# Routing a LoRA gate: one of two small products goes through DRAM, the other takes the whole array in float32r

## The chip, the cores and the metric

The kernel runs on one core of one Trainium2 chip. The core has a matrix engine (TensorE, PE in the profile, with its weight loads under PEld), VectorE (DVE), ScalarE (ACT), GpSimd (POOL) and SyncE (SP), which here does nothing but issue transfers in order. The metric is the time of one execution on the device, in microseconds (us).

## The reference, cut to what matters

For 128 slices x of 128 tokens by 1024 features the reference computes a graph attention step and then a LoRA mixture of experts, each added to its input:

```python
x = x + gnn(layernorm(x), adj, adj, W, a)
x = x + ffn(layernorm(x), router_w, lora_down, lora_up)
# gnn: Wh = h @ W per head (16 heads of 64); att = softmax over columns of
#      leaky_relu(Wh1 + Wh2), masked by adj == 0, times adj; elu(att @ Wh)
# ffn, E = 8 experts of rank R = 16, the 2 best of each slice by its first token:
gates = softmax(top2(y[:, 0, :] @ router_w.T))          # one pair per slice
down = einsum('blh,erh->bler', y, lora_down)
out  = y + einsum('bler,ehr,be->blh', down, lora_up, gates)   # y is the layernorm
```

Each slice uses two experts, and so 2 x 16 = 32 of the 128 LoRA rows. Which two, and with which weights, is known only at run time.

## The kernel before, in words

The slices are taken in 64 pairs (index `q`) and in 32 groups of 4 slices (index `g`, two pairs each). For each pair `project` (L390) computes the product with W in seven products of halves (Strassen's scheme with shared sums), each of 8 float32 matmuls of 128x128 by 260 columns, all on line L417, into two double banks of PSUM. The loop from L835 puts the work of the other stages into eight gaps before, between and after these seven products: every engine gets its instructions in exactly the order in which this loop calls the functions; no scheduler changes it. The gaps hold, for the pair before, the attention (`attend` L534 on TensorE, `update` L544 to L553 on VectorE and ScalarE), its statistics, and the transposing of its result: `turn` copies it into `halves` on ScalarE (L584) and SyncE issues a transposing transfer into `tt` (L586); `rejoin` (L590) copies `tt` into `y_t`.

The expert stage runs per group. In the first of a group's rounds `logits` (L614, L617) multiplies the group's four first tokens by the router, and `choose` finds the two best experts on VectorE. In its second round:

- `fetch` (gap 0, ahead of the first product) tells every LoRA row's partition its expert. The partition's number is 32 x slice + 16 x choice + rank, and the experts' numbers stand on four partitions, one per slice. `spread` (L649) puts them on the diagonal of a 4 x 8 array, and `to_rows` (L670) multiplies ones (4 x 128) by it, so that all eight numbers of the group reach all 128 partitions in `pb`. A mask `slot` (L672) and a sum (L674) pick a partition's own. From `pb` come eight columns of row numbers (L682) for the eight gathers of `down` and one (L685) for the gather of `up`, all on GpSimd (L688, L692).
- `weigh` (end of gap 0) turns the two logits into two gates per slice, on four partitions (L661 to L663), and spreads them in the same way.
- `gates` (gap 3, between the third and the fourth product) takes them to the 128 partitions by a second product on L670, with mask and sum.
- `ffn_down` (gap 4, L707) multiplies the gathered rows by `y_t`, and ScalarE reads the result out into `dn`, times the gate of each partition (L713). `ffn_up` (gaps 5 and 6, L723) multiplies `dn` by the gathered `up`; VectorE adds it to x (L727), and SyncE stores the slice (L730).

So both users of L670 stand in TensorE's stream between products of L417: the first between the seventh product of one pair and the first of the next, the second between the third and the fourth. Tiles of the tag `hp` (`hp`, `halves`, `nz`) share two buffers, and PSUM tiles of the tag `pm` (`pl`, `pb`, `ph`, `pd`, `pu`) four. On SyncE's queue a round begins with the loads of the next pair (L101 for `xt`, L96 for x), then come the two transposes of L586, and then the stores. The last group takes another way (`down_dense`, `gates_dense`, `up_dense`) that uses neither product of L670, so there are 31 of each.

Of the kernel before, what the change touches and what calls it, by code (L numbers as in the profile page):

```python
# [8 lines left out]
F32 = mybir.dt.float32  # L9
F32R = mybir.dt.float32r  # L10
# [4 lines left out]
ALU = mybir.AluOpType  # L15
AX = mybir.AxisListType
# [9 lines left out]
def adj_ffn_kernel(  # L26
# [15 lines left out]
    nc = tc.nc  # L42
    B, N, D = x.shape
    P = 128
# [6 lines left out]
    R = ER // E  # L51
    TOP = 2
    GR = TOP * R
    HALF = 512
# [3 lines left out]
    NG, _, G, _ = adj.shape  # L58
# [5 lines left out]
    const = ctx.enter_context(tc.tile_pool(name="const", bufs=1))  # L64
    work = ctx.enter_context(tc.tile_pool(name="work", bufs=2))
    small = ctx.enter_context(tc.tile_pool(name="small", bufs=3))
    ps_w = ctx.enter_context(tc.tile_pool(name="ps_w", bufs=2, space=bass.MemoryType.PSUM))
    ps_m = ctx.enter_context(tc.tile_pool(name="ps_m", bufs=4, space=bass.MemoryType.PSUM))
# [7 lines left out]
    GRP = {}  # L76


    dram = ctx.enter_context(tc.tile_pool(name="dram", bufs=1, space=bass.MemoryType.DRAM))
# [63 lines left out]
    mean_of, sum_of = (work.tile([P, P], F32, tag="dn", name=n) for n in ("mean_of", "sum_of"))  # L143
# [6 lines left out]
    ident = const.tile([P, P], F32, name="ident")  # L150
# [2 lines left out]
    nc.vector.memset(half_pow, -0.5)  # L153
    fold = small.tile([P, H], F32, tag="fold", name="fold", bufs=1)
    nc.vector.tensor_reduce(fold, ident.rearrange("p (t h) -> p h t", t=KH)[:, 0:H], AX.X, ALU.add)
    ones_g = const.tile([G, P], F32, name="ones_g")
    nc.vector.memset(ones_g, 1.0)

    order = const.tile([G, E], F32, name="order")
    for e in range(E):  # L160
# [121 lines left out]
    slot = down_row = up_row = None  # L282

    def experts(part):

        nonlocal slot, down_row, up_row
        pr = ps_m.tile([P, HALF], F32, tag="pm", name="pr")
        nc.tensor.matmul(pr[:, 0:E + ER], sum_of, part, start=True, stop=True)
        for t, lo, n in ((router_sb.rearrange("p k e -> p e k"), 0, E),
                         (down_sb.rearrange("p e r k -> p (e r) k"), E, ER)):  # L290
            nc.vector.tensor_tensor(t, t, pr[:, lo:lo + n, None].to_broadcast([P, n, KC]),
                                    ALU.subtract)
        nc.sync.dma_start(table.rearrange("(e p) c -> p e c", p=P),
                          down_sb.rearrange("p e r k -> p e (r k)"))

        slot = const.tile([P, 1, G * TOP], F32, name="slot")
        nc.vector.tensor_reduce(slot[:, 0], ident.rearrange("p (j r) -> p j r", r=R), AX.X,
                                ALU.add)
        rows = work.tile([P, P], I32, tag="hp", name="rows")
        nc.gpsimd.iota(rows, pattern=[[0, G * TOP], [1, R]], base=E * R, channel_multiplier=0)  # L300
        at_r = work.tile([P, P], F32, tag="hp", name="at_r")
        nc.vector.tensor_tensor(at_r, rows, ident, ALU.mult)
        up_row = const.tile([P, 1], F32, name="up_row")
        nc.vector.tensor_reduce(up_row, at_r, AX.X, ALU.add)
        row = small.tile([P, 1], I32, tag="row", name="row", bufs=1)
        nc.gpsimd.iota(row, pattern=[[0, 1]], base=E * P, channel_multiplier=1)
        down_row = const.tile([P, 1], F32, name="down_row")
        nc.vector.tensor_copy(down_row, row)
# [311 lines left out]
    def choose(g):  # L620

        st = GRP[g]
        both = small.tile([G, E + 1], F32, tag="lg", name="lg")
        nc.vector.tensor_copy(both, st["pl"][:G, 0:E + 1])
        lg, dev = both[:, 0:E], both[:, E:E + 1]
        top = small.tile([G, 8], F32, tag="top", name="top")
        nc.vector.max(out=top, in_=lg)

        val = small.tile([G, 2, TOP], F32, tag="val", name="val")
        first = small.tile([G, E], F32, tag="first", name="first")  # L630
        mark = small.tile([G, 2, E], F32, tag="mark", name="mark")
        for s in range(TOP):
            nc.vector.scalar_tensor_tensor(mark[:, s], lg, top[:, s:s + 1], order,
                                           op0=ALU.is_equal, op1=ALU.mult)
            if s:
                nc.vector.tensor_scalar(first, order, val[:, 0, 0:1], None, op0=ALU.is_equal)
                nc.vector.scalar_tensor_tensor(mark[:, s], first, float(-E), mark[:, s],
                                               op0=ALU.mult, op1=ALU.add)
            nc.vector.tensor_reduce(val[:, 0, s:s + 1], mark[:, s], AX.X, ALU.max)
        if g < NG - 1:  # L640
            st["experts"] = spread(val[:, 0], "experts")
        pr = small.tile([G, 2], F32, tag="pr", name="pr")
        nc.vector.tensor_sub(pr[:, 0:1], top[:, 1:2], top[:, 0:1])
        st.update(val=val, pr=pr, dev=dev)

    def spread(val, name):

        own = small.tile([G, G, TOP], F32, tag=name, name=name)
        nc.vector.tensor_tensor(own, ident[:G, :G, None].to_broadcast([G, G, TOP]),  # L649
                                val[:, None, :].to_broadcast([G, G, TOP]), ALU.mult)  # L650
        return own.rearrange("g t s -> g (t s)")

    def ratio(g):
        st = GRP[g]
# [2 lines left out]
    def weigh(g):  # L657

        st = GRP[g]
        gate, pr = st["val"][:, 1], st["pr"]  # L660
        nc.vector.tensor_scalar(gate[:, 0:1], pr[:, 1:2], 1.0, None, op0=ALU.add)  # L661
        nc.vector.reciprocal(gate[:, 0:1], gate[:, 0:1])
        nc.vector.tensor_mul(gate[:, 1:2], pr[:, 1:2], gate[:, 0:1])  # L663
        if g < NG - 1:
            st["gates"] = spread(gate, "gates")

    def to_rows(own, name):

        pb = ps_m.tile([P, HALF], F32, tag="pm", name="pb")
        nc.tensor.matmul(pb[:, 0:G * TOP], ones_g, own, start=True, stop=True)  # L670
        mine = small.tile([P, G * TOP], F32, tag="mine", name="mine")
        nc.vector.tensor_tensor(mine, pb[:, 0:G * TOP], slot[:, 0], ALU.mult)  # L672
        of_slot = small.tile([P, 1], F32, tag=name, name=name)
        nc.vector.tensor_reduce(of_slot, mine, AX.X, ALU.add)  # L674
        return pb, of_slot

    def fetch(g):

        st = GRP[g]
        pb, mine = to_rows(st["experts"], "of_slot")  # L680
        at_down = small.tile([P, G * TOP], U32, tag="at_down", name="at_down")
        nc.vector.tensor_scalar(at_down, pb[:, 0:G * TOP], float(-P), down_row, op0=ALU.mult,  # L682
                                op1=ALU.add)
        at_up = small.tile([P, 1], U32, tag="at_up", name="at_up")
        nc.vector.tensor_scalar(at_up, mine, float(-R), up_row, op0=ALU.mult, op1=ALU.add)  # L685
        st["down"] = work.tile([P, G * TOP * R, KC], F32, tag="down", name="down", bufs=1)
        for j in range(G * TOP):
            nc.gpsimd.indirect_dma_start(  # L688
                out=st["down"][:, j * R:(j + 1) * R].rearrange("p r k -> p (r k)"), out_offset=None, in_=table,
                in_offset=bass.IndirectOffsetOnAxis(ap=at_down[:, j:j + 1], axis=0))  # L690
        st["up"] = work.tile([P, D], F32, tag="up", name="up", bufs=1)
        nc.gpsimd.indirect_dma_start(  # L692
            out=st["up"], out_offset=None, in_=up_t,
            in_offset=bass.IndirectOffsetOnAxis(ap=at_up[:, 0:1], axis=0))

    def gates(g):

        st = GRP[g]
        st["gate"] = to_rows(st["gates"], "gate")[1]

    def ffn_down(g):

# [132 lines left out]
    for q in range(NQ + 2):  # L835
        gaps = [[] for _ in range(8)]
        if q == 0:
            prepare(gaps)
        g, part = divmod(q - 2, 2)
        ffn = 0 <= g < NG  # L840
        if ffn and not part:
            gaps[6] += [(logits, g), (choose, g)]
# [3 lines left out]
        if ffn and not part:  # L846
            gaps[6].append((ratio, g))
            if g == NG - 1:
                gaps[6] += [(down_dense, g, 3, 1), (weigh, g)]
# [27 lines left out]
        if ffn and part and g == NG - 1:  # L877
            gaps[0] += [(gates_dense, g), (up_dense, g)]
        elif ffn and part:
            gaps[0].insert(0, (fetch, g))  # L880
            gaps[0].append((weigh, g))
            gaps[3].insert(0, (gates, g))
            gaps[4].insert(0, (ffn_down, g))
            gaps[5].insert(0, (ffn_up, (g, 0)))
            gaps[6].append((ffn_up, (g, 1)))
# [14 lines left out]
        if q == 1:  # L900
            gaps[0].append((squares_of, 1))
            gaps[5].append(keep("tables", table_parts))
            gaps[7].append(keep("", experts, "tables"))
# [50 lines left out]
```

## Time and profile before

| | |
|---|---|
| time, median of 3 runs | 1949.1 us (1949.08 to 1950.11) |
| span of the profiled run | 1947.3 us |
| TensorE busy | 1931.7 us, 99% |
| VectorE busy | 1638.3 us, 84% |
| ScalarE busy | 1089.6 us, 56% |
| GpSimd busy | 832.7 us, 43% |
| TensorE's share of the chain that ended last | 95% |
| granted clock of TensorE | 0.996 of full |

A line of the profile's groups gives the source line, the engine, the operation, output and input, the array's rows and columns in use for a matmul, the moving operand's shape, then the count, the busy time in us, the mean ns of one, and the idle time of the engine just before them with what ended it. A line of the timeline gives the start in us, how long a run of equal instructions took, the instruction, how many of it were merged, and in brackets the idle time before it. Matmuls overlap in their pipeline: the time of one record is a latency, and the distance from one to the next is what it costs.

### The profile page before, as it was taken

To read this page: it belongs to the slowest core of one execution; us is meant where nothing else is said; L and a number is where in the kernel's file an instruction comes from. 1 tells how busy PE (TensorE), PEld (TensorE's weight loads), DVE (VectorE), ACT (ScalarE), POOL (GpSimd) and SP (SyncE) were. 2 spreads that over 40 slices of the span, in tenths; PEclk is the share of its full clock that TensorE was granted. 3 is DMA by queue.
4 is the path that set the end of the run, shared out by engine and by line. 5 is a ranking of instruction groups with operands and counts; after the bars stand their busy time and mean duration, and the time that the engine had idled before them with its cause. 6 is when DMAs were issued, how large, how long until landed. Compare 5 with 4: busy or idle time off the path is not lost.

```text
span 1947.3 us, 30291 instructions
## 1 busy us (share of the span) xinstructions
PE 1931.7 (99%) x11096; PEld 1574.6 (81%) x11096; DVE 1638.3 (84%) x3477; ACT 1089.6 (56%) x1060; POOL 832.7 (43%) x1135
## 2 busy tenths in 40 slices
PE   9999999999999999999999999999999999999997
PEld 6878888888888888888888888888888888888885
DVE  6888888888988888888888888888888888888886
ACT  3656556556555556555555565565555555555653
POOL 3345433355444355333454433553444553334540
PEclk9999999999999999999999999999999999999998
DMA  7455655665655656556557556556556565565452
GB/s 302 133 184 142 183 172 153 187 176 136 197 175 152 190 151 164 182 159 179 184 130 194 171 151 188 167 148 193 170 163 185 146 174 176 154 187 182 125 165 95
DMA packets 343955, 329.25 MB, mean 169 GB/s; under 512 B 274304, under 2 KB 276352, under 8 KB 343296
## 3 DMA queue, kind: packets, MB, share of 16 engines
q1 hardware_dynamic: 326080, 285.35, 50.1%
q0 software_dynamic: 17008, 40.91, 7.3%
q8 instruction: 88, 1.44, 0.3%
q10 hardware_dynamic: 720, 1.06, 0.1%
q14 instruction: 59, 0.48, 0.1%
HBM read 193.57 MB, written 67.63 MB: 134 GB/s over the span
## 4 chain that ended last, share of the span: by engine, by line
PE 95%; DVE 2%; ACT 1%; DMA 0%; issue 0%; POOL 0%; POOLq 0%; DVEq 0%; ACTq 0%
PE pw L417 80%; PE ph L534 6%; PE pu L723 3%; PE pd L707 3%; PE pb L670 1%; PE pl L614 1%; PE pu L784 1%; DMA tt<-halves 0%; DVE xn L553 0%; DVE hp L544 0%; DVE xn L552 0%; PE idle L149 0%; DVE stats L314 0%; ACT xn L606 0%; DVE parts L490 0%
## 5 line engine op out<-in xcount | busy, mean ns | idle before, releaser
L417 PE MATMUL pw<-w_sb,xt 128*128 128x260 f32 (+1 forms) x4080 | 944.4, 386 | 0.0
L417 PEld LDWEIGHTS pw<-w_sb,xt 128*128 128x128 f32 x4080 | 764.7, 190 | 144.7 <-issue 24.6
L417 PE MATMUL pw<-w_sb,s 128*128 128x260 f32 (+1 forms) x3072 | 711.1, 384 | 1.9 <-DVE u L425 1.9
L417 PEld LDWEIGHTS pw<-w_sb,s 128*128 128x128 f32 x3072 | 578.1, 190 | 115.7 <-issue 22.8
L318 POOL TENSOR_SCALAR rstd<-mv 128x2 f32<-128x2 f32 x126 | 27.4, 218 | 851.3 <-DVE mv L315 846.1
L590 ACT COPY y_t<-tt 128x2048 uint16<-128x2048 uint16 x126 | 313.1, 2505 | 67.3 <-DMA tt<-halves 67.1
L688 POOL DMA_INDIRECT down<-table,at_down x248 | 251.5, 1014 | 163.0 <-DVE e L508 89.4
L314 DVE BATCH_NORM_STATS2 stats<-xn 128x6 f32<-128x512 f32 x504 | 318.8, 674 | 0.1
L584 ACT COPY halves<-xn 128x2048 uint16<-128x2048 uint16 x126 | 239.3, 1899 | 141.0 <-DVE xn L553 141.0
L486 ACT ACTIVATE parts<-wh,rstd 128x512 fp32r<-128x512 f32 x192 | 134.1, 716 | 213.8 <-DVE wh L425 213.8
L551 ACT ACTIVATE ex<-hp 128x1024 f32<-128x1024 f32 x128 | 135.3, 1057 | 177.4 <-DVE hp L544 177.4
L727 DVE SCALAR_TENSOR_TENSOR xn<-pu,rstd,xn 128x512 f32<-128x512 f32 x248 | 169.0, 744 | 21.9 <-PE pu L723 21.9
L544 DVE TENSOR_TENSOR hp<-ph,att 128x512 f32<-128x512 f32 x256 | 161.3, 671 | 10.3 <-PE ph L534 10.0
L553 DVE SCALAR_TENSOR_TENSOR xn<-ex,xn 128x1024 f32<-128x1024 f32 x128 | 156.8, 1225 | 14.2 <-DVE xn L552 0.9
L534 PE MATMUL ph<-parts,adj_f 128*128 128x512 f32 x512 | 164.5, 443 | 1.3 <-ACT parts L486 0.8
L425 DVE TENSOR_TENSOR wh<-pw,u 128x520 f32<-128x520 f32 (+1 forms) x128 | 89.1, 696 | 90.0 <-PE pw L417 86.6
L552 DVE SCALAR_TENSOR_TENSOR xn<-hp,xn 128x1024 f32<-128x1024 f32 x128 | 156.8, 1225 | 4.4
L606 ACT ACTIVATE xn<-xn,off,mul 128x1024 f32<-128x1024 f32 x128 | 151.3, 1231 | 1.5 <-POOL off L571 1.5
L490 DVE SCALAR_TENSOR_TENSOR parts<-wh,rstd,parts 128x512 fp32r<-128x512 f32 x192 | 137.8, 745 | 11.1 <-ACT parts L486 11.1
L534 PEld LDWEIGHTS ph<-parts,adj_f 128*128 128x128 f32 x512 | 96.6, 189 | 20.9 <-ACT parts L486 1.2
L425 DVE TENSOR_TENSOR wh<-pw,p 128x520 f32<-128x520 f32 (+1 forms) x64 | 44.7, 699 | 81.6 <-PE pw L417 81.6
L319 POOL TENSOR_TENSOR rstd<-rstd,half_pow 128x2 f32<-128x2 f32 x126 | 89.7, 712 | 10.5
(156 smaller groups left out, 1485.0 us busy)
## 6 DMA issues: line engine op xcount, KB each, us to landing
xn<-in_x SPq DMA_DIRECT2D x128, 512.0 KB, 6.6
xt<-in_x_t SPq DMA_DIRECT2D x127, 512.0 KB, 5.6
out_y<-xn SPq DMA_DIRECT2D x124, 512.0 KB, 3.9
adj_f<-in_adj_t POOLq DMA_DIRECT2D x32, 256.0 KB, 3.0
adj_i<-in_adj SPq DMA_DIRECT2D x32, 256.0 KB, 2.6
down<-table,at_down POOLq DMA_INDIRECT x248, 3.9
w_sb<-in_w SPq DMA_DIRECT2D x3, 1040.0 KB, 10.6
wt_sb<-in_w_t SPq DMA_DIRECT2D x1, 2048.0 KB, 18.1
```

Source lines behind the costliest of these rows:

```text
L314: nc.vector.bn_stats(st[:, h, :], X[i][:, h * HALF:(h + 1) * HALF])
L417: nc.tensor.matmul(dst[:, j, cols], lhs[:, k, :], w_sb[:, rhs, k, j, cols], start=(first and k == 0), stop=(k == KH - 1), skip_group_check ...
L490: nc.vector.scalar_tensor_tensor(in_two(PARTS[q][:, 1, b]), block, rstd, in_two(PARTS[q][:, 0, b].bitcast(F32)), op0=ALU.mult, op1=ALU.sub ...
L534: nc.tensor.matmul(PH[i][h], GRP[g]["adj_f"][:, t, :], PARTS[q][:, s, NH * (i % 2) + h], start=(s == 0), stop=(s == 1))
L544: nc.vector.tensor_tensor(hp[:, h * HALF:(h + 1) * HALF].rearrange("p (h f) -> p h f", f=F), ph.rearrange("p (h f) -> p h f", f=F), att[:, ...
L552: nc.vector.scalar_tensor_tensor(xt, hp, 0.0, xt, op0=ALU.max, op1=ALU.add)
L553: nc.vector.scalar_tensor_tensor(xt, ex, 1.0, xt, op0=ALU.min, op1=ALU.add)
L584: nc.scalar.copy(halves, X[i].bitcast(U16).rearrange("p (d s) -> p s d", s=2))
L590: nc.scalar.copy(y_of(i).bitcast(U16).rearrange("p k (n s) -> p s k n", s=2), TT.pop(i).rearrange("p (s k) n -> p s k n", s=2))
L606: nc.scalar.activation(X[i], X[i], AF.Identity, bias=GRP[g]["off"][:, t:t + 1], scale=GRP[g]["mul"][:, t:t + 1])
L688: nc.gpsimd.indirect_dma_start(out=st["down"][:, j * R:(j + 1) * R].rearrange("p r k -> p (r k)"), out_offset=None, in_=table, in_offset=b ...
L727: nc.vector.scalar_tensor_tensor(y[:, cols], pu[t], st["rstd"][:, t:t + 1], y[:, cols], op0=ALU.mult, op1=ALU.add)
```

## The change

Two things change in how numbers reach the partitions of the LoRA rows. The gates are no longer multiplied by ones: `put_away` repeats each gate 16 times along a row (4 x 32), SyncE writes these 128 numbers to a small array in DRAM, and `of_rows` reads them back one per partition (128 x 1). The experts still go through a product, but its operands now fill all 128 rows of the array (the ones are 128 x 128, and the diagonal array is a constant tile of 128 rows, of which the lower 124 stay zero), and both are float32r. It is meant to take work off TensorE's stream.

The diff, cut to what the steps speak of:

```diff
-    ones_g = const.tile([G, P], F32, name="ones_g")
-    nc.vector.memset(ones_g, 1.0)
+    ones_r = const.tile([P, P], F32R, name="ones_r")
+    nc.vector.tensor_scalar(ones_r, mean_of, float(D), None, op0=ALU.mult)
+    spread = const.tile([P, G, TOP], F32R, name="spread")
+    nc.vector.memset(spread.bitcast(F32), 0.0)
...
         if g < NG - 1:
-            st["experts"] = spread(val[:, 0], "experts")
+
+            nc.vector.tensor_tensor(spread[0:G], ident[:G, :G, None].to_broadcast([G, G, TOP]),
+                                    val[:, None, 0].to_broadcast([G, G, TOP]), ALU.mult)
...
-    def spread(val, name):
-
-        own = small.tile([G, G, TOP], F32, tag=name, name=name)
-        nc.vector.tensor_tensor(own, ident[:G, :G, None].to_broadcast([G, G, TOP]),
-                                val[:, None, :].to_broadcast([G, G, TOP]), ALU.mult)
-        return own.rearrange("g t s -> g (t s)")
+    def put_away(val, name):
+
+        own = small.tile([G, TOP, R], F32, tag="own", name="own", bufs=2)
+        nc.vector.tensor_copy(own, val[:, :, None].to_broadcast([G, TOP, R]))
+        rows = dram.tile([P, 1], F32, tag=name, name=name, bufs=2)
+        nc.sync.dma_start(rows.rearrange("(g r) o -> g (r o)", g=G),
+                          own.rearrange("g s r -> g (s r)"))
+        return rows
+
+    def of_rows(rows, name):
+
+        mine = small.tile([P, 1], F32, tag=name, name=name)
+        nc.sync.dma_start(mine, rows)
+        return mine
...
         if g < NG - 1:
-            st["gates"] = spread(gate, "gates")
-
-    def to_rows(own, name):
-
+            st["gate"] = of_rows(put_away(gate, "gates"), "gate")
+
+    def fetch(g):
+
+        st = GRP[g]
         pb = ps_m.tile([P, HALF], F32, tag="pm", name="pb")
-        nc.tensor.matmul(pb[:, 0:G * TOP], ones_g, own, start=True, stop=True)
-        mine = small.tile([P, G * TOP], F32, tag="mine", name="mine")
-        nc.vector.tensor_tensor(mine, pb[:, 0:G * TOP], slot[:, 0], ALU.mult)
-        of_slot = small.tile([P, 1], F32, tag=name, name=name)
-        nc.vector.tensor_reduce(of_slot, mine, AX.X, ALU.add)
-        return pb, of_slot
-
-    def fetch(g):
-
-        st = GRP[g]
-        pb, mine = to_rows(st["experts"], "of_slot")
+        every = pb[:, 0:G * TOP]
+        nc.tensor.matmul(every, ones_r, spread.rearrange("p g s -> p (g s)"), start=True,
+                         stop=True)
+        own = small.tile([P, G * TOP], F32, tag="own_slot", name="own_slot", bufs=1)
+        nc.vector.tensor_tensor(own, every, slot, ALU.mult)
+        mine = small.tile([P, 1], F32, tag="of_slot", name="of_slot", bufs=1)
+        nc.vector.tensor_reduce(mine, own, AX.X, ALU.add)
...
-    def gates(g):
-
-        st = GRP[g]
-        st["gate"] = to_rows(st["gates"], "gate")[1]
...
         elif ffn and part:
             gaps[0].insert(0, (fetch, g))
             gaps[0].append((weigh, g))
-            gaps[3].insert(0, (gates, g))
```

More of the change, by code (lines that the diff above doesn't have):

```diff
@@ L294, in experts @@
                           down_sb.rearrange("p e r k -> p e (r k)"))
-        slot = const.tile([P, 1, G * TOP], F32, name="slot")
-        nc.vector.tensor_reduce(slot[:, 0], ident.rearrange("p (j r) -> p j r", r=R), AX.X,
-                                ALU.add)
+        slot = const.tile([P, G * TOP], F32, name="slot")
+        nc.vector.tensor_reduce(slot, ident.rearrange("p (j r) -> p j r", r=R), AX.X, ALU.add)
         rows = work.tile([P, P], I32, tag="hp", name="rows")
@@ L664, in weigh @@
         if g < NG - 1:
-            st["gates"] = spread(gate, "gates")
-    def to_rows(own, name):
-        pb = ps_m.tile([P, HALF], F32, tag="pm", name="pb")
-        nc.tensor.matmul(pb[:, 0:G * TOP], ones_g, own, start=True, stop=True)
-        mine = small.tile([P, G * TOP], F32, tag="mine", name="mine")
-        nc.vector.tensor_tensor(mine, pb[:, 0:G * TOP], slot[:, 0], ALU.mult)
-        of_slot = small.tile([P, 1], F32, tag=name, name=name)
-        nc.vector.tensor_reduce(of_slot, mine, AX.X, ALU.add)
-        return pb, of_slot
+            st["gate"] = of_rows(put_away(gate, "gates"), "gate")
     def fetch(g):
         st = GRP[g]
-        pb, mine = to_rows(st["experts"], "of_slot")
+        pb = ps_m.tile([P, HALF], F32, tag="pm", name="pb")
+        every = pb[:, 0:G * TOP]
[5 more added lines that the diff above has]
+        nc.vector.tensor_reduce(mine, own, AX.X, ALU.add)
         at_down = small.tile([P, G * TOP], U32, tag="at_down", name="at_down")
-        nc.vector.tensor_scalar(at_down, pb[:, 0:G * TOP], float(-P), down_row, op0=ALU.mult,
+        nc.vector.tensor_scalar(at_down, every, float(-P), down_row, op0=ALU.mult,
                                 op1=ALU.add)
```

## The prediction

> **What bounds the kernel now.** I read the busy shares and the chain that ended last first, from the page.
>
> ```profile
> PE 1931.7 (99%) x11096; PEld 1574.6 (81%) x11096; DVE 1638.3 (84%) x3477; ACT 1089.6 (56%) x1060; POOL 832.7 (43%) x1135
> ...
> PE 95%; DVE 2%; ACT 1%; DMA 0%; issue 0%; POOL 0%; POOLq 0%; DVEq 0%; ACTq 0%
> PE pw L417 80%; PE ph L534 6%; PE pu L723 3%; PE pd L707 3%; PE pb L670 1%; PE pl L614 1%; PE pu L784 1%; DMA tt<-halves 0%; DVE xn L553 0%; DVE hp L544 0%; DVE xn L552 0%; PE idle L149 0%; DVE stats L314 0%; ACT xn L606 0%; DVE parts L490 0%
> ```
>
> TensorE sets the end: 99% busy and 95% of the chain. Time taken out of its stream is time taken off the kernel, unless another engine makes it wait. The edited line, L670, is 1% of the chain. Next, the groups of TensorE with shapes kept apart:
>
> ```profile
> L417 PE MATMUL pw<-w_sb,xt 128*128 128x260 f32 x4032 | 932.9, 386 | 0.0
> ...
> L534 PE MATMUL ph<-parts,adj_f 128*128 128x512 f32 x512 | 164.5, 443 | 1.3 <-ACT parts L486 0.8 <-DVE parts L490 0.5
> ...
> L670 PE MATMUL pb<-experts,ones_g 4*128 4x8 f32 x62 | 11.9, 262 | 0.0
> L670 PE MATMUL pb<-gates,ones_g 4*128 4x8 f32 x62 | 11.9, 262 | 0.0
> ```
>
> The records say how many passes a matmul takes. L417 runs 63 rounds x 7 products x 8 matmuls = 3528 float32 matmuls, and leaves 7056 records (4032 here, 3024 with `s`): two each. L670 has two each as well (31 groups, 62 records). L534, whose operands are float32r, has 128 slices x 4 = 512 matmuls and 512 records: one each. "4*128" is rows by columns of the array: L670 is a product over 4 rows, all its neighbours use 128.
>
> The mean of 262 ns is the latency of one record. What a product costs is how far it pushes the next one back, and that stands in TensorE's timeline, once around the experts' product, once with the gates', once with neither:
>
> ```profile
> 990.68 0.38 PE L417 MATMUL pw<-w_sb,xt 128*128 128x260 f32 x1
> 990.99 0.38 PE L670 MATMUL pb<-experts,ones_g 4*128 4x8 f32 x2
> 991.31 0.71 PE L417 MATMUL pw<-w_sb,xt 128*128 128x260 f32 x2
> ...
> 1000.29 3.67 PE L417 MATMUL pw<-w_sb,xt 128*128 128x260 f32 x16
> 1003.89 0.38 PE L670 MATMUL pb<-gates,ones_g 4*128 4x8 f32 x2
> 1004.20 3.77 PE L417 MATMUL pw<-w_sb,s 128*128 128x260 f32 x16
> 1007.91 1.99 PE L707 MATMUL pd<-y_t,down 128*32 128x128 f32 x64
> ...
> 1031.86 3.67 PE L417 MATMUL pw<-w_sb,xt 128*128 128x260 f32 x16
> 1035.36 3.67 PE L417 MATMUL pw<-w_sb,s 128*128 128x260 f32 x16
> ```
>
> Undisturbed, 16 records start every 3.50 us (1031.86 to 1035.36), 219 ns each. Around the experts' product the last record before it ends at 990.68 + 0.38 = 991.06, the second after it at 991.31 + 0.71 = 992.02: 0.96 us for two records that take 2 x 0.219 = 0.44 alone. So pb costs about 0.52. The single records, to the ns, split it: 312 ns from the last pw start to the first pb start instead of 219 (93 more), 133 ns to the second pb, 180 ns to the next pw, and 324 ns to the one after that instead of 219 (105 more): 93 + 133 + 180 + 105 = 511 ns. All 62 products of L670 show the same steps within a few ns. L670 thus costs 62 x 0.511 = 31.7 us, more than the 23.8 us that its two rows are busy.
>
> **What the Trainium skill says.** "TensorEngine Tiling (Array Packing)", Key Properties: changing the tiling mode drains TensorE. The trace agrees: every step from 128x128 to pb, pd, pu or pl takes 312 or 313 ns between starts, and the first pb weight load starts together with its matmul, while L534's weights (128x128) load during the record before. "TensorE: Matmul & The Clock Gate", Part 2, step 1: the next weights load while the present matmul runs, and the load's time follows columns, not rows. It agrees: pb's loads take 182 ns with 4 rows, pw's 190 with 128. "DMA: Bandwidth & Descriptors", Anatomy of one DMA: about 2 us fixed per transfer, most of it the wait until the write is confirmed (fitted for GpSimd's path); in the same page "Two DMAs through the same engine are not ordered", so the read-back must wait for the write's completion. Here the 256 KB adj_i load lands in 2.6 us, the 8 KB a_cols in 3.2. No page prices a float32r matmul.
>
> **The change part by part.** *The gates' product goes*, with its mask and sum. TensorE: 31 x 0.511 = 15.8 us, all on the path, since pw before it and pw after it then join at 219 ns.
>
> *The experts' product at 128 rows and in float32r.* The two drains (93 and most of 105) go with the change of array shape, and one pass of two goes. What stays is a matmul of 8 columns, too short to hide the next pw's weight load. Nearest row: L274, 128x128 with 16 columns.
>
> ```profile
> L274 PE MATMUL ps<-fold,part x4: 179/262/263, 45.7 to 45.9; 128*128 128x16 f32 x4
> ```
>
> Its passes follow each other at 111 ns in the records, the pace of weight loads, and the pw after them is 97 ns late; its first pass adds 16 ns to the end of the pw before. So one pass costs about 16 + 97 = 0.11 us. L534 shows that float32 to float32r and back adds nothing at this shape (pw after ph ends 219 ns later, as ever)[...]. I take 0.12. Lower end 0.08, if the weight load hides in part; upper end 0.40, if only the second pass (112 ns) goes and the drains stay. Saving 0.511 - 0.12 = 0.39, x 31 = 12.1 us.
>
> *VectorE.* Gone per group: mask 154 ns and sum 161 ns of the gates. L649's spread stays for the experts (now into 4 rows of a constant tile) and becomes a 4x32 copy for the gates, priced as L649's 154 ns. Net 0.3 us less. None of it counts: VectorE waits for TensorE in each of these rounds.
>
> *Constants at the start.* A 128x128 scaling and a memset of 128x8 against a memset of 4x128, 0.2 us each at most (memset of 128x128: 165 ns), ahead of the 2.0 us in which VectorE waits for a_cols: nothing.
>
> *Two transfers per group on SyncE's queue*, 512 B out, 512 B back. They stand behind the round's x loads and ahead of its two transposes, as SyncE's timeline of one such round shows; VectorE's and ScalarE's of the same round follow.
>
> ```profile
> 991.13 0.80 SPq L101 DMA_DIRECT2D xt<-in_x_t  x2
> 991.99 0.90 SPq L96 DMA_DIRECT2D xn<-in_x  x2
> 1001.65 8.49 SPq L586 DMA_TRANSPOSE tt<-halves  x2
> ```
>
> ```profile
> 995.73 0.15 DVE L649 TENSOR_TENSOR gates<-ident,val 4x8 f32<-4x8 f32 x1
> ...
> 1013.63 0.70 DVE L425 TENSOR_TENSOR wh<-pw,u 128x520 f32<-128x520 f32 x1 [2.40 <-PE pw L417]
> ```
>
> ```profile
> 1005.51 1.90 ACT L584 COPY halves<-xn 128x2048 uint16<-128x2048 uint16 x1 [0.71 <-DVE xn L553]
> 1009.96 0.37 ACT L713 ACTIVATE dn<-pd,gate 128x128 f32<-128x128 f32 x1 [2.55 <-PE pd L707]
> ```
>
> The gates are ready at 995.9, SyncE issues the write at about 996.0. At 2.6 us it lands at 998.6, the read at 1001.2; the queue is free before the transposes want it at 1001.65. At the worst landing in this stretch, xn's 7.0 us, the write lands at 1003.0, the read (3.2) at 1006.2, and the transposes start 1.4 us late. Who waits: `dn` (L713) needs the gate at 1009.96, some 0.9 us earlier once TensorE is ahead: 1009.06, so the gate is 3 to 8 us early. Behind late transposes stands ScalarE's second `halves` copy (its buffer is freed by the first transpose): 1.4 us late it ends at 8.8 instead of 7.4 past 1000, still ahead of 9.06. After that, pu has all of the next product (3.5 us) before it wants dn. So the transfers cost nothing, in either bound.
>
> Would another engine stop TensorE once it is 0.9 us ahead in this round? The banks of pw are read 3.3 us or more before they are written again (product 7 starts at 1009.82, its bank is free at 1006.14; VectorE idles 2.40 us before 1013.63). The tight place is pl, in the other round of a group: TensorE loses 1.5 us there in all waiting for ScalarE's y_t. The chain into it (ph, hp, xn, halves, tt, y_t) starts from ph of that same round, which has no pb, so it moves with TensorE and gains no wait.
>
> **Sum:** 15.8 + 12.1 = 27.9 us; 1949.1 - 27.9 = 1921.2.
>
> **Rivals.**
> - *The new product keeps much of its cost*: the drains come from the wait on VectorE or from the short matmul, not from the array's shape. For: pb's first load carries a semaphore wait. Against: L534's loads carry such waits too and are pulled ahead. Saving 31 x (0.511 + 0.112) = 19.3, time 1929.8.
> - *The saved time is given back at pl or in a bank wait.* For: VectorE is busy 84% and pl already waits now and then. Against: the slacks above. All given back: 1949; half: 1935.
> - *SyncE's wait for the write holds the transposes back* and the kernel is slower. Beyond about 5 us of lateness (1.65 of ScalarE's wait plus 3.2 of pu's) every us costs 31; the saving of 0.9 per group is gone at about 6. With 7 us it ends near 1921 + 62 = 1983. For: the wait stands in order ahead of transposes that ScalarE waits for. Against: it needs the write to take over 10 us, where 7.0 is the longest landing in this stretch.
>
> **How the numbers follow.** Forecast 0.84, the first rival 0.07, given back in part or in full 0.06 (in full: 0.01), slower 0.03. The range: low, pb at 0.08 saves 31 x (0.511 + 0.431) = 29.2, 1919.9, less the 1.0 us by which the runs of before differ, 1918.9; high, pb at 0.26, midway to its upper end, saves 31 x (0.511 + 0.251) = 23.6, 1925.5, plus 1.0, 1926.5. Faster 0.84 + 0.07 + 0.05 = 0.96, same 0.01, slower 0.03.
>
> **What would show it.** Right: no gates' product between the third and fourth product, so these two start 3.50 us apart; a single 128*128 pb record per group, and the pw records around it pushed apart by 0.11 to 0.13 us over their 219 ns; SyncE's transposes at the same distance from `halves`; `dn` still waiting for pd and not for a transfer. Wrong: `dn` waiting on the gate's DMA, a new wait of `halves` on the transposes, or 312 ns between pw and pb as now.

## The result, and the profile after

The changed kernel takes 1921.8 us (median of 4 runs, 1919.6 to 1923.5) against 1949.15 before (1949.08 to 1950.11): a ratio of 0.9858, 95% interval 0.9841 to 0.9875. The forecast was 1921.2. Run again later, beside a kernel before of 1948.7, it took 1923.2 (1918.5 to 1926.1), a ratio of 0.9874 (0.9859 to 0.9889).

The page after, busy shares and chain:

```profile
PE 1903.6 (99%) x11003; PEld 1565.7 (82%) x11003; DVE 1630.6 (85%) x3416; ACT 1088.3 (57%) x1060; POOL 832.2 (43%) x1135
...
PE 91%; DVE 4%; ACT 2%; DMA 2%; issue 1%; POOL 0%; DVEq 0%; POOLq 0%; ACTq 0%
```

TensorE lost 28.1 us of busy time and 93 records (62 of the gates, 31 second passes of the experts) and is still the bound. The chain that ended last now runs 4% over VectorE, 2% over ScalarE and 2% over transfers, where it had 3% of VectorE and ScalarE and next to none of transfers: in some groups `pl` waits for `y_t`, and there the chain goes back over `tt` and `halves`. TensorE's groups after have one line of pb left, where there were two:

```profile
L683 PE MATMUL pb<-spread,ones_r 128*128 128x8 f32 x31 | 11.2, 360 | 0.0
```

The mean of a record went up from 262 to 360 ns. A product now has one record and had two that overlap, so its busy time only went from 11.9/31 = 0.38 to 11.2/31 = 0.36 us: read alone, this line would call the new product hardly cheaper. The distance to its neighbours says otherwise, in TensorE's timeline after:

```profile
977.46 0.60 PE L418 MATMUL pw<-w_sb,xt 128*128 128x260 f32 x2
977.70 0.36 PE L683 MATMUL pb<-spread,ones_r 128*128 128x8 f32 x1
977.92 0.69 PE L418 MATMUL pw<-w_sb,xt 128*128 128x260 f32 x2
...
986.88 3.67 PE L418 MATMUL pw<-w_sb,xt 128*128 128x260 f32 x16
990.39 3.67 PE L418 MATMUL pw<-w_sb,s 128*128 128x260 f32 x16
993.99 1.99 PE L710 MATMUL pd<-y_t,down 128*32 128x128 f32 x64
```

The pw before pb ends at 977.46 + 0.60 = 978.06, pb at 977.70 + 0.36 = 978.06 as well, the second pw after it at 977.92 + 0.69 = 978.61: 0.55 us where two pw take 0.44. Before it was 0.96. Between the third and the fourth product nothing stands any more: 986.88 to 990.39, one product's pace. In all 31 groups the single records put pb's end some 6 ns after the pw before it, and the end of the next pw 325 ns after that instead of 219: 6 + 106 = 112 ns per product, where each of the two products of before cost 511. (The profile models the ends of TensorE's records. Sums from an undisturbed pw to the next come out the same by starts; how a sum splits into going in and coming back rests on the ends.)

SyncE's queue in the same round, then ScalarE's dn:

```profile
978.12 0.80 SPq L101 DMA_DIRECT2D xt<-in_x_t  x2
978.98 0.92 SPq L96 DMA_DIRECT2D xn<-in_x  x2
982.92 0.27 SPq L654 DMA_DIRECT2D gates<-own  x1
987.40 0.33 SPq L661 DMA_DIRECT2D gate<-gates  x1
988.65 7.70 SPq L587 DMA_TRANSPOSE tt<-halves  x2
```

```profile
986.72 1.90 ACT L585 COPY halves<-xn 128x2048 uint16<-128x2048 uint16 x1 [1.53 <-DVE xn L554]
...
996.04 0.37 ACT L716 ACTIVATE dn<-pd,gate 128x128 f32<-128x128 f32 x1 [1.63 <-PE pd L710]
```

The write takes SyncE's queue from 982.92 to 987.40, and the first transpose starts 0.03 us after halves is ready (986.72 + 1.90 = 988.62), as in every such round of before and after. Every one of the 31 dn still waits for pd, none for a transfer. The list of waits gives what waited, for what, the us in all, how often, and the longest:

```profile
ACT dn L716 <- PE pd L710: 51.2, 31, 2.2
```

### The profile page after: what moved, and what is told of

Read it like the earlier page. It is cut to its first block, busy times and chain, and to the rows that moved or that the text cites. A ratio compares the mean times of both kernels' runs of the same rounds, so it can differ in the third digit from the quotient of the medians.

```text
span 1920.7 us, 30166 instructions
## 1 busy us (share of the span) xinstructions
PE 1903.6 (99%) x11003; PEld 1565.7 (82%) x11003; DVE 1630.6 (85%) x3416; ACT 1088.3 (57%) x1060; POOL 832.2 (43%) x1135
## 4 chain that ended last, share of the span: by engine, by line
PE 91%; DVE 4%; ACT 2%; DMA 2%; issue 1%; POOL 0%; DVEq 0%; POOLq 0%; ACTq 0%
PE pw L418 77%; PE ph L535 6%; PE pu L726 3%; PE pd L710 3%; DMA tt<-halves 1%; PE pl L615 1%; ACT y_t L591 1%; DVE xn L554 1%; ACT halves L585 1%; DVE xn L553 1%; DVE hp L545 1%; DVE stats L315 1%; PE pu L787 0%; DMA down<-table,at_down 0%; PE idle L149 0%
## 5 line engine op out<-in xcount | busy, mean ns | idle before, releaser
L418 PE MATMUL pw<-w_sb,xt 128*128 128x260 f32 (+1 forms) x4080 | 939.2, 385 | 0.0
L418 PEld LDWEIGHTS pw<-w_sb,xt 128*128 128x128 f32 x4080 | 764.4, 190 | 144.9 <-issue 24.9
L418 PE MATMUL pw<-w_sb,s 128*128 128x260 f32 (+1 forms) x3072 | 709.6, 384 | 1.9 <-DVE u L426 1.9
L418 PEld LDWEIGHTS pw<-w_sb,s 128*128 128x128 f32 x3072 | 581.9, 190 | 117.4 <-POOL xt L371 22.8
L319 POOL TENSOR_SCALAR rstd<-mv 128x2 f32<-128x2 f32 x126 | 27.4, 218 | 824.8 <-DVE mv L316 819.6
```

What stands on the lines that cost most here:

```text
L418: nc.tensor.matmul(dst[:, j, cols], lhs[:, k, :], w_sb[:, rhs, k, j, cols], start=(first and k == 0), stop=(k == KH - 1), skip_group_check ...
```

## The experiments

The first four kernels ran side by side on one chip beside a kernel before of 1948.8 us, the next four beside one of 1947.7, the last two beside one of 1948.7. Across the three sets the ratios are what compares. Each edit is shown as a diff against the changed kernel, and cut.

**One half alone: the gates through DRAM.** The experts' product stays as it was, over 4 rows in float32.

```diff
-    ones_r = const.tile([P, P], F32R, name="ones_r")
-    spread = const.tile([P, G, TOP], F32R, name="spread")
+    ones_r = const.tile([P, P], F32, name="ones_r")
+    spread = const.tile([P, G, TOP], F32, name="spread")
...
-        nc.tensor.matmul(every, ones_r, spread.rearrange("p g s -> p (g s)"), start=True,
-                         stop=True)
+        nc.tensor.matmul(every, ones_r[0:G], spread[0:G].rearrange("p g s -> p (g s)"),
+                         start=True, stop=True)
```

> The gates go through DRAM; the experts' product stays over 4 rows in float32. Account by steps: the gates' product cost TensorE 0.511 us per group and the transfers cost nothing, so 31 x 0.511 = 15.8 us less than before, 1933.3 us. Rival, the transfers cost something that the whole change hides in its gain: above 1935, with ScalarE's dn or halves waiting on a transfer.

Measured: 1933.2 us (1930.0 to 1934.1), ratio 0.9922 (0.9908 to 0.9936), 15.6 us below the before of its chip. The remaining product shows 312, 133 and 181 ns between starts, as before.

**The other half alone: the experts' product.** The gates' product stays over 4 rows in float32, with its own constant tile `spread_g` and `ones_g`, and no transfer is made.

```diff
-            st["gate"] = of_rows(put_away(gate, "gates"), "gate")
+            nc.vector.tensor_tensor(spread_g[0:G], ident[:G, :G, None].to_broadcast([G, G, TOP]),
+                                    gate[:, None, :].to_broadcast([G, G, TOP]), ALU.mult)
...
+        nc.tensor.matmul(pb[:, 0:G * TOP], ones_g[0:G], spread_g[0:G].rearrange("p g s -> p (g s)"),
+                         start=True, stop=True)
...
+            gaps[3].insert(0, (gates, g))
```

> The experts' product over 128 rows in float32r; the gates' product stays over 4 rows in float32, no transfer. Account by steps: 0.511 - 0.112 = 0.399 us less per group, x 31 = 12.4, 1936.8 us. With the run of the gates alone the two savings then add up to 28.2 us. Rival, the two products' savings are not independent (what one gives the other takes): this one gives under 8 us, above 1941.

Measured: 1936.0 us (1935.2 to 1937.9), ratio 0.9939 (0.9926 to 0.9953), 12.8 us below. In one and the same trace the two kinds stand side by side: pb over 128 rows in float32r adds 112 ns, pb over 4 rows in float32 adds 511. Together the halves save 15.6 + 12.8 = 28.4 us, where the account by steps has 28.2. Each of the two has an interval of about 2.7 us either way, so nothing speaks for one taking from the other, though a loss of up to about 4 us would not show in these times.

**Which of the two did it, the array's rows or float32r?** Two kernels, each with one of them. First 128 rows in float32:

```diff
-    ones_r = const.tile([P, P], F32R, name="ones_r")
-    spread = const.tile([P, G, TOP], F32R, name="spread")
-    nc.vector.memset(spread.bitcast(F32), 0.0)
+    ones_r = const.tile([P, P], F32, name="ones_r")
+    spread = const.tile([P, G, TOP], F32, name="spread")
+    nc.vector.memset(spread, 0.0)
```

> The changed kernel with the experts' product over 128 rows, but in float32. If the array's shape made the two drains, they stay away, and only the second pass comes back at the pace of a weight load, 0.11 us: 0.22 us per product, 31 x 0.11 = 3.4 us above the changed kernel, 1925.2. Rival, float32r and not the shape removed the drains: 0.40 us per product, 8.9 us above, 1930.7; then TensorE's records show 312 ns from pw to pb again.

Measured: 1925.25 us (1924.75 to 1925.81), ratio 0.9882 (0.9867 to 0.9897). Then 4 rows in float32r:

```diff
-        nc.tensor.matmul(every, ones_r, spread.rearrange("p g s -> p (g s)"), start=True,
-                         stop=True)
+        nc.tensor.matmul(every, ones_r[0:G], spread[0:G].rearrange("p g s -> p (g s)"),
+                         start=True, stop=True)
```

> The changed kernel with the experts' product over 4 rows, in float32r. If the shape makes the drains they are back, one pass of 112 ns less than before: 0.40 us per product, 31 x 0.29 = 8.9 us above the changed kernel, 1930.7, with 312 ns from pw to pb. Rival, float32r removed them: as the changed kernel, 1921.8.

Measured: 1929.6 us (1927.7 to 1930.7), ratio 0.9900 (0.9885 to 0.9915). TensorE's timeline of the first, then of the second, around the experts' product:

```profile
976.03 3.77 PE L418 MATMUL pw<-w_sb,xt 128*128 128x260 f32 x16
979.64 0.28 PE L683 MATMUL pb<-spread,ones_r 128*128 128x8 f32 x2
979.78 3.75 PE L418 MATMUL pw<-w_sb,xt 128*128 128x260 f32 x16
983.18 1.28 PE L535 MATMUL ph<-parts,adj_f 128*128 128x512 f32 x4
```

```profile
979.25 3.77 PE L418 MATMUL pw<-w_sb,xt 128*128 128x260 f32 x16
982.96 0.27 PE L683 MATMUL pb<-spread,ones_r 4*128 4x8 f32 x1
983.16 3.77 PE L418 MATMUL pw<-w_sb,xt 128*128 128x260 f32 x16
986.58 1.28 PE L535 MATMUL ph<-parts,adj_f 128*128 128x512 f32 x4
```

The two times are 4.4 us apart and their intervals overlap, so the traces must decide. From the first pw to ph these are 7.15 and 7.33 us. In the single records the first product costs 10 + 111 + 103 = 224 ns, the second 198 + 198 = 396. The step from pw to pb is 219 ns between starts over 128 rows in float32, and 312 over 4 rows in float32r, in all 31 groups of each: the drain belongs to the rows. With the run of the gates alone (4 rows in float32, 511 ns) and the changed kernel (128 rows in float32r, 112 ns) all four combinations are measured. Counted between ends and in float32r, going into pb adds 198 ns over 4 rows and 6 over 128; coming back to pw adds 198 and 106. What stays at 128 rows, the 106 ns, is close to the 110 ns at which the weight loads follow each other just there (the record of one load lasts 190 ns). That it is a weight load which the short matmul can't hide fits this, but no run tests it. float32r itself takes out one pass of 111 ns. Rows first, then float32r: 511 - 224 = 287 and 224 - 112 = 112 ns.

**Both products over 128 rows in float32r, no transfer.** As the second experiment, but with `spread_g` of 128 rows in float32r, and `ones_r` in place of `ones_g`:

```diff
+        nc.tensor.matmul(pb[:, 0:G * TOP], ones_r, spread_g.rearrange("p g s -> p (g s)"),
+                         start=True, stop=True)
```

> Both products over 128 rows in float32r, no transfer for the gates. Account by steps: each costs 0.112 us instead of 0.511, so 31 x 2 x 0.399 = 24.7 us less than before, 1924.3, or 3.5 us above the changed kernel. Rival, the transfers are not free: then this is level with the changed kernel (1921.8) or faster.

Measured: 1922.8 us (1922.6 to 1925.2), ratio 0.9876 (0.9860 to 0.9893): 24.9 us less than before by the medians, as the account has it. The 3.5 us by which the account puts it above the changed kernel are not resolved by the times: the intervals of the two ratios overlap, and the changed kernel's second run (0.9874) lies level with it. So the times alone leave the rival open, too; the middle stretch at the end of this section sets it against the records. Most of what the change saves was to be had without the way through DRAM.

**No round trip at all.** The gates' product and transfers both go.

```diff
+    half_gate = const.tile([P, 1], F32, name="half_gate")
+    nc.vector.memset(half_gate, 0.5)
...
-            st["gate"] = of_rows(put_away(gate, "gates"), "gate")
+            st["gate"] = half_gate
```

> The changed kernel with the gates of the first 31 groups left out: dn is scaled by a constant 0.5, with neither a product nor a transfer. It is the price of the round trip through DRAM taken alone. If the round trip is hidden, as the changed kernel within its spread, 1920 to 1923. Rival, SyncE's wait for the write or the late gate costs something: below 1918.

Measured: 1921.8 us (1920.9 to 1922.4), ratio 0.9866 (0.9850 to 0.9883), between the changed kernel's two. The round trip costs nothing that these times can resolve, which is some 3 us.

**How far from costing something? One, three and five more hops.** Each hop is a DRAM to DRAM copy of the 128 numbers, issued by SyncE once the one before has landed.

```diff
-            st["gate"] = of_rows(put_away(gate, "gates"), "gate")
+            rows = put_away(gate, "gates")
+            hop0 = dram.tile([P, 1], F32, tag="hop0", name="hop0", bufs=2)
+            nc.sync.dma_start(hop0, rows)
...
+            st["gate"] = of_rows(hop0, "gate")
```

> The gates go through a second array in DRAM (write, DRAM to DRAM, read). SyncE is held some 2.5 us longer, so the transposes start 1 to 2 us late and the gate lands some 3 us ahead of dn. By the slack worked out (about 5 us of lateness before TensorE waits) the time is as that of the changed kernel, 1920 to 1924. Rival, there is no such slack and every us of lateness is paid: 1.4 x 31 = 43 us more, near 1965.

> The gates go through three more arrays in DRAM one after the other. SyncE is held some 7.5 us longer and the transposes start some 6 us late, past the slack of about 5 us. Then ScalarE's second halves copy, dn behind it and pu wait, 1.5 us or more per group: 1968 or above. Rival, the transfers are not on any path at all: as the changed kernel.

> The gates go through five more arrays in DRAM. With three more, 19 of 31 dn already waited for the gate and the shortest distance from dn's end to pu was 0.41 us of 3.2. Two more hops take some 3.8 us, so the gate lands 2 to 4 us after pd and past pu's place: TensorE waits 1 us or more before pu in each group, and the time goes to 1955 or above. Rival, the round trip was never near a path and more hops change nothing: 1922 to 1925.

| more hops | us | ratio to before | write to read issued, median us | first transpose after halves, median us | dn that wait for the gate |
|---|---|---|---|---|---|
| 0 (first run) | 1921.8 | 0.9858 | 3.5 | 0.03 | 0 of 31 |
| 1 | 1923.6 | 0.9879 (0.9863 to 0.9896) | 5.3 | 0.09 | 0 |
| 3 | 1924.3 | 0.9881 (0.9864 to 0.9897) | 9.4 | 4.2 | 19 |
| 5 | 1995.9 | 1.0238 (1.0224 to 1.0252) | 14.6 | 9.4 | 29 |

One and three more hops lie within the spread of the changed kernel's two runs, so the forecast of 1968 for three was wrong. For one thing the transposes came 4.2 us late (median), not 6, which is still inside the 5 us that the account allowed. For another, the account had the path wrong, as ScalarE's timeline with three more hops tells:

```profile
987.43 1.90 ACT L585 COPY halves<-xn 128x2048 uint16<-128x2048 uint16 x1 [1.53 <-DVE xn L554]
...
993.22 1.90 ACT L585 COPY halves<-xn 128x2048 uint16<-128x2048 uint16 x1 [0.84 <-DVE xn L554]
996.71 0.37 ACT L723 ACTIVATE dn<-pd,gate 128x128 f32<-128x128 f32 x1 [1.59 <-DMA gate<-hop]
1000.19 4.87 ACT L591 COPY y_t<-tt 128x2048 uint16<-128x2048 uint16 x2 [3.11 <-DMA tt<-halves]
```

SyncE's of the same round:

```profile
993.86 0.34 SPq L661 DMA_DIRECT2D gate<-hop  x1
994.32 5.75 SPq L587 DMA_TRANSPOSE tt<-halves  x2
```

The second halves copy starts at 993.22, before the first transpose is even issued at 994.32. It does not wait for that transpose's buffer. In the built program, where each tile's address can be read, the second halves of a round takes the buffer of the hp just before it, so the chain that I had put between the transposes and dn does not exist. Of the transfers dn waits for the gate's alone, and it has pu's 3.2 us to lose (from dn's end to pu's start, before and after). With five more hops that is spent. TensorE's timeline of one group there, and its ScalarE's:

```profile
1021.64 1.99 PE L721 MATMUL pd<-y_t,down 128*32 128x128 f32 x64
1023.55 3.77 PE L418 MATMUL pw<-w_sb,xt 128*128 128x260 f32 x16
1028.57 1.14 PE L737 MATMUL pu<-up,dn 32*128 32x512 f32 x8 [1.24 <-ACT dn L727]
...
1062.17 0.55 PE L615 MATMUL pl<-router_sb,y_t 128*4 128x8 f32 x16 [0.80 <-ACT y_t L591]
```

```profile
1028.15 0.37 ACT L727 ACTIVATE dn<-pd,gate 128x128 f32<-128x128 f32 x1 [5.74 <-DMA gate<-hop]
1031.18 4.83 ACT L591 COPY y_t<-tt 128x2048 uint16<-128x2048 uint16 x2 [2.66 <-DMA tt<-halves]
```

dn comes 3.6 us (median) after pd's end, pu waits for it, and one round later pl waits for y_t, in all 31 groups. A third wait follows: in some groups a product of L418 waits for VectorE's `parts`. TensorE's longest waits there:

```profile
PE pl L615 <- ACT y_t L591: 26.6, 31, 1.2
PE pu L737 <- ACT dn L727: 16.1, 18, 1.8
PE pw L418 <- DVE parts L491: 13.1, 11, 1.4
```

Beside the changed kernel of the same chip it loses 1995.9 - 1923.2 = 72.6 us, 2.3 per group.

**The changed kernel again.**

> The changed kernel again, beside the one above on the same chip: 0.9858 of before as in its first run, within 0.002; the split experiments are set against it.

Measured: 1923.2 us (1918.5 to 1926.1), ratio 0.9874 (0.9859 to 0.9889), within the 0.002 named.

**The middle stretch alone.** The first 100 us and the last 65 together take 3.9 us longer in the first profile of the changed kernel than in the second. So I take from each profile the time from the first start of the experts' product to its last, 30 groups on, and the sum of the 30 steps between ends from pw to pl.

| kernel | stretch, us | pw to pl, us |
|---|---|---|
| before | 1776.4 | 3.4 |
| changed, first and second profile | 1750.4, 1750.3 | 4.6, 4.6 |
| gates through DRAM alone | 1761.7 | 4.2 |
| experts' product alone | 1764.9 | 3.9 |
| 128 rows in float32 | 1753.6 | 4.5 |
| 4 rows in float32r | 1760.3 | 6.2 |
| both products, no transfer | 1752.8 | 3.5 |
| no round trip | 1750.3 | 4.2 |
| one, three, five more hops | 1750.6, 1751.6, 1813.8 | 4.0, 5.2, 30.8 |

The two profiles of the changed kernel agree to 0.1 us; of the others there is one each. The two halves of the change save 14.8 and 11.5 us here, 26.3 together, and the whole change 26.0 and 26.1. Both products at 128 rows take 2.4 us longer than the changed kernel here: 30 x 0.112 = 3.4 for the product, less 1.1 at pl. So the way through DRAM is the better one by that much, and the rival of that run, that its transfers cost something, finds nothing here: without the round trip the stretch is the same to 0.2 us, and three more hops cost 1.2. Among the kernels that compute the whole result none is shorter here than the changed one.

## Why the prediction was right, point by point

- *TensorE is the bound, and a product costs what it pushes its neighbours apart.* Right. 62 x 0.511 = 31.7 us before, 31 x 0.112 = 3.5 after: 28.2 us by the records. The two runs give 27.4 and 25.5 by the medians. In the middle stretch the account asks for 30 x (0.511 + 0.399) = 27.3, and the two profiles give 26.0 and 26.1.
- *The gates' product, 15.8 us.* Measured alone at 15.6.
- *The experts' product, 0.39 us per group, 12.1 us.* Measured alone at 12.8, and 0.399 by the records. The nearest row, L274, gave 16 + 97 = 113 ns where 6 + 106 = 112 were measured: each part was off by 9 or 10 ns, and that they cancel is luck. Rounding it up to 0.12 was not needed.
- *The drains go with the change of the array's shape.* Shown by the two split kernels; the first rival, that they come from the wait or from the short matmul, had 312 ns at any shape and falls. The split by starts, 93 + 133 + 180 + 105, was a poor guide to what would stay; counted between ends it is 198 going in and 198 coming back for one pass, of which 192 and 92 went.
- *The transfers are hidden.* Right in its outcome: leaving them out changes nothing, by the times or in the middle stretch. Its working had two terms off. The write was put at 2.6 us, up to 7.0; from its issue to the read's issue it takes 3.5 (1.2 to 4.6), still ahead of the transposes, but in the round shown by only 0.9 us (the read's issue ends at 987.73). And the slack behind it rested on halves waiting for the first transpose, which the run with three more hops refutes. In that run transposes 4.2 us late cost next to nothing; with five more hops, 9.4 us late and with the gate behind pu's place, 2.3 us per group are lost, where the rival's rule (every us beyond 5 is paid) asks for 4.4. What the late transposes cost and what the late gate costs were not told apart beyond that.
- *The saved time is not given back.* Nearly right. In the middle stretch 1.2 to 1.3 us of the 27.3 are missing, and the steps from pw to pl, which the prediction expected to gain no wait, grew by 1.2. They are 3.4 to 3.9 us in the three kernels that keep a product for the gates and 4.0 or more in all that have none, the one without transfers among them. So the wait seems to come with the product's going and not with the transfers; the margin is small, there is one profile of most kernels, and why it should, no run here shows.
- *The total, 1921.2.* That it met the first run's 1921.8 so closely is partly chance: the second run gave 1923.2, and the start and the end of a run alone move the total by more than the difference.

## What to carry to other kernels

On a saturated TensorE, price a small matmul by the distance between its neighbours' ends, not by its own duration: here the cheaper product had the longer record. A product over 4 rows among products over 128 costs two changes of shape; padding it with zeros to the neighbours' shape is worth more (287 ns) than a cheaper number format (112 ns), and a few numbers can go through DRAM instead where enough time lies between their maker and their user (here some 13 us from the write to dn, for a round trip whose write alone takes 3.5). Whether a wait in a transfer queue is harmless is best found by lengthening it until it costs.

## What the runs showed that was not expected

TensorE can run at half its pace for a few us after a short wait. In all twelve profiles a wait of 1.85 us for VectorE ends at 28.5 to 29.2 us. In the changed kernel's first profile the records after it come at 427 ns instead of 216, from 30.1 to 33.5 us, and the granted clock is half; in its second profile they don't. Of the twelve profiles three show it (the other two: 128 rows in float32, and no round trip). Why only these is not shown. The stretch from 27 to 34 us, of the first and of the second (columns: stretch, us, TensorE busy and its records, granted clock, DMA share, GB/s):

```profile
27.00:34.00 7.00, 5.29 (x16) 0.76 1.04 404
```

```profile
27.00:34.00 7.00, 5.24 (x32) 1.00 1.05 405
```

The same busy time holds 16 records or 32. By the single records it costs 8 x 0.21 = 1.7 us, as much as many of the differences above. At the end it is the same: over the last 30 us the granted clock is 0.75 of full in the profile of before and 0.83 and 0.94 in the two of the changed kernel. These stretches are one reason why whole times of kernels that differ by 3 us stay unresolved.

Each dependent DRAM to DRAM copy of 512 B holds the next transfer of SyncE's queue back by 1.9 us (median; 1.75 to 4.7), where in the profile of before a load of 256 KB lands in 2.6.
